# Moving a filter check into a hand-ordered instruction table, and giving the first tables a tile of their own

## The chip, the cores and the metric

The kernel runs on one core of one Trainium2 chip, as a single launch. The metric is the device time of the launch in microseconds (us). Engines are named as in the profile: PE (matmul), PEld (its weight loads), DVE (vector), ACT (scalar), POOL (gpsimd) and SP, whose queue issues most of the DMAs.

## The reference, cut to what matters

Two layers work on `x` of 4 x 32 images of 128 x 128, in float32. Four images are the batch, 32 the tokens.

```python
x = x + L0_conv(_ln_c(x))     # attention over 32 tokens, 16 heads, in a truncated Fourier basis,
                              # then two spectral mixers with instance norms
t = tokens(x)
t = t + L0_ffn(_ln_t(t))      # sigmoid recurrence over 128*128 rows, with batch statistics
x = from_tokens(t)
x = x + L1_conv(_ln_c(x))     # below
t = tokens(x)
t = t + L1_ffn(_ln_t(t))

def _ln_c(v):
    return (v - mean(v, -1)) / sqrt(var(v, -1) + 1e-6)

def _L1_conv_ref(x, bias, up_filter, dn_filter):
    x = x + bias
    x = repeat(repeat(x, 2, axis=2), 2, axis=3)
    x = conv_same(x, up_filter)               # 12 x 12 taps
    x = leaky_relu(x, 0.2) * sqrt(2)
    x = conv_same(x, dn_filter)               # 12 x 12 taps
    return x[:, :, ::2, ::2]
```

The two filters come in as 12 x 12 arrays. The kernel's convolution stage uses them as products of a column and a row. `filters()` checks on the chip that each filter is such a product (the result goes to `ok`, which is read at the end and would start a general path, not used here) and writes the one-dimensional taps to a small DRAM tensor `hankel`, from which the convolution stage builds its band matrices.

## The kernel before

**Stages.** The image array `XA` stays in SBUF (8 MB). In order of time:

- 0 to 137 us: loading, the row statistics and normalisation of `_ln_c`, the transform of every image to 32 x 17 coefficients, the scores of the attention and their softmax. There are eight steps `k`, each half a batch image set (16 tokens of one batch entry): `stats(k, n)` (DVE `bn_stats` L823, then `row_stats` L382 to L390, `rsqrt_of` L372 to L380, `p_n` at L829), `normalise` (ACT L845, DVE L847), `transform(k)` (PE L862 with the table of columns, L870 and L874/L876 with the tables of rows), then `scores` (ps_fr L895, FK L902, the products KM L909, psc L936) and `attend` (L1001 to L1020). Normalised images are stored to DRAM (`normed`, L881) and loaded again at L1071.
- 137 to 200 us: sums over tokens (`pm` L1092, `df` L1286), then norms.
- 200 to 449 us: the mixers, in eight chunks of four tokens.
- 449 to 505 us: the first recurrence; then the convolution stage, and the second recurrence with the output.

**Tables of constants.** `cst` is one tile of 128 partitions. SP loads it with two DMAs: the first 354 columns (`C_E`, `C_DW`, `C_CR`, which the transform uses) at L590 after two loads of `x`, the other 713 columns at L604 after two more. After them come the other loads of `x`, then `md` (a small bounce through DRAM that replicates the query-key weights, L653 and L655), and further weights.

**The one-column instruction.** `ndcm` (L717) is 1 - `dcm`, one column of the second part of `cst`. It is written in `weights()` after a piece of its own, and the scheduler put it between L379 and L380 of the first statistics.

**Orders.** Inside `with in_order():` every engine runs its instructions in the order in which the program makes them; outside (steps k = 2 to 7) a scheduler chooses. `SUMS`, `NORMS`, `MIXERS` are tables of names `piece.chunk`, run inside `in_order()`. The pieces of the mixers that matter here:

- `Z` (L1418, DVE: reads the first mixer's inverse from PSUM), `g` (L1423, ACT: gelu), `ST` (L1429, PE), `A` (L1434, ACT), `PF` (L478, PE, 32 matmuls), `ZS` (L1453, DVE statistics of Z), `ZD` (L1457 to L1459, DVE)
- `M1`, `PS`, `M2`, ..., `M4c` (L1565, L1566, DVE: the coefficients `G`), `FHG` (L491, PE: 64 small matmuls on `G`), `GB`/`gBc` (L1553, L1556), `IRI`/`IRS` (L506, PE), `TA` (L1579, PE), `R` (L1586 and L1587, DVE: the residual sums into `XA`)
- `FS` (L1597, DVE statistics for the first recurrence), `AF` (eight small operations from L1609, on POOL for most chunks; for the last chunk two `row_stats` of eight columns on DVE), `PW` (L1622, POOL power), `AO` (L1626), `XN`, `XT`, `XC`, `WX`, `BN` (the recurrence's inputs)

A name with two numbers, as `R1b.2`, is a part of a piece and its chunk. Bank "t" of the PSUM pool `psf` has one buffer, which `PS`, `GB` and `XT` take in turn.

**The filters before.** `filters()` (L739 to L808) is a generator of nine pieces, two times four and a DMA. Each half is: five DVE operations on 7 partitions (`fsq` to `frows`, L759 to L765); two matmuls `ps_f` on PE (L769, L770) and the copy `sums` on DVE (L772); eight DVE operations (`total` to `ok`, L775 to L785); six or seven (`fv` to `taps`, L789 to L805). The ninth is the POOL DMA `hankel<-taps` (L807). It was run as `extra` among the pieces of the last batch's scores:

```python
for work in (scoring, extra, extra, extra, scoring, scoring, scoring, products, products, scoring, scoring,
             scoring, scoring, scoring, extra, extra, scoring):
    step(work)
through(scoring, extra, attend(NB - 1))
```

`big("ps_f")` takes one of three PSUM buffers that the scores share.

Of the kernel before, what the change touches and what calls it, by code (L numbers as in the profile page):

```python
# [32 lines left out]
P = 128  # L33
# [5 lines left out]
PAD = 3  # L39
# [115 lines left out]
    IRI0.2 M4b.1 de.1 M4c.1 FHG.1 gBc.1 g3.2 Z0.2 FS2.0 Z1.2 g2.2 QG0.1 FS1.0 FS0.0 g1.2 g0.2 ST2.2 A2.2 sq2.2 FS3.0  # L155
    IRS0.1 TA1.1 ZS2.2 AF.0 sq3.2 ST0.2 QG1.1 PW.0 ZS3.2 ZD.2 A0.2 TA0.1 PF.2 sq0.2 R1a.1 sq1.2 LD2.1 FZ.2 SQ.2
    R0b.1 R0a.1 FHIa.3 R1b.1 AO.0 IRS2.1 M1.2 TA2.1 LD0.2 FHIb.3 R2b.1 XN1a.0 XN0b.0 PS.2 M2.2 TA3.1 QI0.3 XN0a.0
    PG1.2 XN1b.0 QI1.3 R2a.1 PG2.2 XT0.0 M2b.2 IRI2.3 R3a.1 R3b.1 XC0.0 XT1.0 P2.2 IRI0.3 Z2.3 M3.2 Z3.3 WX0.0 XC1.0
    P3.2 XN2a.0 al.2 Z0.3 M4a.2 g2.3 M4b.2 g3.3 Z1.3 g0.3 de.2 GB.2 M4c.2 BN0.0 g1.3 FS2.1 FS1.1 ZS2.3 ST2.3 sq1.3
    sq2.3 FHG.2 ST0.3 QG0.2 XN3b.0 IRS0.2 A2.3 A0.3 TA1.2 gBc.2 TA0.2 XN2b.0 FS3.1 PF.3 sq0.3 FS0.1 WC0.0 XT2.0  # L160
    ZS3.3 QG1.2 sq3.3 WX1.0 FZ.3 ZD.3 R1b.2 AF.1 R0b.2 IRS2.2 SQ.3 TA3.2 XC2.0 PW.1 R0a.2 PG1.3 R1a.2 M1.3 BN1.0
    LD2.2 PS.3 TA2.2 R3a.2 XN3a.0 WC1.0 M2.3 AO.1 WX2.0 R2a.2 FHIa.4 BN2.0 R3b.2 PG2.3 XN0b.1 FHIb.4 M2b.3 XT3.0
    P2.3 XN0a.1 M3.3 WC2.0 al.3 QI0.4 R2b.2 QI1.4 P3.3 XC3.0 IRI0.4 XN1a.1 XT0.1 Z1.4 M4a.3 IRI2.4 WX3.0 XN1b.1 Z0.4
    XC0.1 g1.4 M4b.3 de.3 g0.4 M4c.3 Z3.4 Z2.4 GB.3 FHG.3 BN3.0 FS3.2 g3.4 FS1.2 FS2.2 LD0.3 QG0.3 ST0.4 g2.4 FS0.2
    gBc.3 A0.4 QG1.3 ZS3.4 ZS2.4 IRS0.3 sq1.4 TA1.3 sq2.4 ST2.4 LD2.3 R1a.3 TA0.3 A2.4 WC3.0 PF.4 R1b.3 XN2b.1 FZ.4
    AF.2 ZD.4 XT1.1 sq3.4 R0b.3 WX0.1 IRS2.3 PW.2 R0a.3 SQ.4 sq0.4 PG1.4 TA2.3 XC1.1 M1.4 PS.4 BN0.1 TA3.3 AO.2 M2.4
    M2b.4 R2b.3 XN3a.1 XN2a.1 WC0.1 XT2.1 FHIa.5 R3b.3 LD0.4 R3a.3 XC2.1 P2.4 XN3b.1 XN0b.2 M3.4 PG2.4 XN0a.2 P3.4
    FHIb.5 QI0.5 QI1.5 XT3.1 WX1.1 IRI0.5 al.4 R2a.3 XN1a.2 XC3.1 BN1.1 M4a.4 Z1.5 IRI2.5 de.4 WC1.1 M4b.4 M4c.4
    XN1b.2 FS0.3 GB.4 gBc.4 WX2.1 XT0.2 BN2.1 g1.5 XN2b.2 Z3.5 WC2.1 FHG.4 FS3.3 XC0.2 QG0.4 WX3.1 FS1.3 FS2.3 QG1.4
    LD2.4 XT1.2 XN2a.2 XN3a.2 IRS0.4 XC1.2 TA1.4 BN3.1 Z2.5 TA0.4 AF.3 g2.5 Z0.5 R1b.4 XT2.2 IRS2.4 g0.5 WC3.1  # L170
    FHIa.6 sq0.5 R1a.4 R0a.4 R0b.4 WX0.2 ZS2.5 PW.3 g3.5 ZS3.5 BN0.2 TA2.4 AO.3 FHIb.6 ZD.5 ST2.5 sq2.5 FS0.4 R2b.4
    XN3b.2 ST0.5 XC2.2 sq1.5 R2a.4 sq3.5 WC0.2 A0.5 TA3.4 WX1.2 R3b.4 BN1.2 A2.5 PF.5 QI0.6 IRI0.6 XN0a.3 R3a.4
    XN0b.3 XT3.2 Z0.6 WC1.2 FZ.5 SQ.5 M1.5 QI1.6 PG1.5 XC3.2 g0.6 Z1.6 IRI2.6 PS.5 Z2.6 M2.5 g1.6 WX2.2 Z3.6 g2.6
    g3.6 P2.5 BN2.2 M2b.5 M3.5 XN1a.3 XT0.3 FS2.4 PG2.5 P3.5 FS3.4 XC0.3 ST0.6 al.5 M4a.5 WC2.2 A0.6 ST2.6 de.5
    M4b.5 M4c.5 WX0.3 A2.6 BN0.3 XN1b.3 PF.6 ZS2.6 sq0.6 ZS3.6 sq3.6 FS1.4 GB.5 FZ.6 FHG.5 WC0.3 SQ.6 QG0.5 WX3.2
    sq2.6 AF.4 IRS0.5 TA0.5 PW.4 PG1.6 sq1.6 gBc.5 XT1.3 QG1.5 M1.6 XC1.3 LD0.5 ZD.6 BN3.2 TA1.5 R0a.5 XN2a.3 R0b.5
    PS.6 LD2.5 AO.4 IRS2.5 M2.6 XN3b.3 XN2b.3 TA3.5 WC3.2 XT2.3 P2.6 M2b.6 XN3a.3 WX1.3 XC2.3 R1a.5 PG2.6 XT3.3
    TA2.5 R1b.5 FHIa.7 FHIb.7 XN0a.4 R3a.5 BN1.3 M3.6 R2a.5 XN0b.4 XC3.3 WC1.3 WX2.3 XN1b.4 QI0.7 R2b.5 XT0.4 P3.6
# [12 lines left out]
    XC22.7 WX20.7 BN20.7 WC00.7 WC02.7 WX22.7 BN22.7 WC20.7 WC22.7
# [15 lines left out]
C_E = 0  # L207

C_DW = C_E + 130
C_CR = C_DW + 96  # L210
C_SW = C_CR + 128
C_EH2 = C_SW + 256
# [19 lines left out]
def _constants():  # L232
    c = np.zeros((P, C_N), np.float64)
# [16 lines left out]
    c[:, C_E + 64 : C_E + 128] = rows.real.T @ basis  # L250
    c[:, C_E + 128 : C_E + 130] = (rows.imag.T @ basis)[:, :2]
# [3 lines left out]
    c[:, C_CR : C_CR + 64] = cols.real  # L255
    c[:, C_CR + 64 : C_CR + 128] = -cols.imag
# [30 lines left out]
def _network(  # L287
# [94 lines left out]
    def row_stats(st, n, mean, var):  # L382

        d = sm([P, NG], "rw_d")[:, :n]
        tt(mean, st[:, :, 1], st[:, :, 4], ALU.add)
        ts(mean, mean, 0.5, None, ALU.mult)
        tt(d, st[:, :, 1], st[:, :, 4], ALU.subtract)
        stt(d, d, 0.25, d, ALU.mult, ALU.mult)
        tt(var, st[:, :, 2], st[:, :, 5], ALU.add)
        stt(var, var, 1.0 / P, d, ALU.mult, ALU.add)  # L390
# [169 lines left out]
    s4 = aw.tile([P, NB], F32, name="s4")  # L560
    ndcm = aw.tile([P, 1], F32, name="ndcm")
# [28 lines left out]
    nc.sync.dma_start(cst[:, :C_SW], consts[:, :C_SW])  # L590
# [6 lines left out]
    if redo is not None:  # L597
        for k in range(2):
            F = wp.tile([2 * PAD + 1, 2, 12], F32, name=f"F{k}")
            taps_in.append(F)  # L600
            for j in range(2):
                f = up[j, 0] if k == 0 else dn[j]
                nc.gpsimd.dma_start(F[:, j, :], f[P // 2 - PAD : P // 2 + PAD + 1, :, P // 2])
    nc.sync.dma_start(cst[:, C_SW:], consts[:, C_SW:])  # L604
# [10 lines left out]
    def weights():  # L615
# [101 lines left out]
        ts(ndcm, dcm, -1.0, 1.0, ALU.mult, ALU.add)  # L717
# [21 lines left out]
    def filters():  # L739

        n = 2 * PAD + 1
# [4 lines left out]
        taps = wp.tile([1, 8, n], F32, name="taps")  # L750
        for k in range(2):
            F = taps_in[k]

            def small_(shape, name):
                return wp.tile(shape, F32, tag=name, name=name)


            fsq = small_([n, 3, 12], "fsq")
            tt(fsq[:, 0, :], F[:, 0, :], F[:, 1, :], ALU.add)  # L759
            tt(fsq[:, 1:3, :], F, F, ALU.mult)  # L760
            tt(fsq[:, 1, :], fsq[:, 1, :], fsq[:, 2, :], ALU.add)
            rsum = small_([n, 2], "rsum")
            nc.vector.tensor_reduce(rsum, F, AX.X, ALU.add)
            rows = small_([n, n, 2], "frows")
            tt(rows, ident[0:n, 0:n].unsqueeze(2).broadcast_to([n, n, 2]),  # L765
               rsum.unsqueeze(1).broadcast_to([n, n, 2]), ALU.mult)
            yield True
            p = big("ps_f")
            mm(p[:n, 0:24], ones_sq[0:n, 0:n], fsq[:, 0:2, :].rearrange("p a b -> p (a b)"), start=True, stop=True)  # L769
            mm(p[:n, 24 : 24 + 2 * n], ones_sq[0:n, 0:n], rows.rearrange("p a b -> p (a b)"), start=True, stop=True)  # L770
            sums = small_([n, 24 + 2 * n], "sums")
            nc.vector.tensor_copy(sums, p[:n, : 24 + 2 * n])  # L772
            yield True
            total = small_([n, 2], "total")
            nc.vector.tensor_reduce(total, sums[:, :24].rearrange("p (a b) -> p a b", a=2), AX.X, ALU.add)  # L775
            bound = small_([n, 1], "bound")
            tt(bound, total[:, 0:1], total[:, 0:1], ALU.mult)
            stt(bound, bound, FILTER_TOL * FILTER_TOL, total[:, 1:2], ALU.mult, ALU.mult)
# [1638 lines left out]
```

## Time and profile before

| what | us |
|---|---|
| median of 3 runs (lowest, highest) | 869.35 (868.36, 869.44) |
| profiled execution, its own time | 870.38 |
| its span | 868.6 |
| PE, DVE, ACT, POOL busy | 750.8, 710.9, 649.4, 361.2 |
| mean granted TensorE clock | 0.939 |

| stretch, us | length | PE | DVE | ACT | POOL | DMA share |
|---|---|---|---|---|---|---|
| 0 to 137 | 137 | 94.09 | 95.73 | 81.23 | 8.41 | 0.81 |
| 137 to 200 | 63 | 51.01 | 55.54 | 41.18 | 4.26 | 0.38 |
| 200 to 449 | 249 | 214.59 | 211.66 | 192.27 | 106.80 | 0.25 |
| 449 to 505 | 56 | 51.69 | 52.67 | 52.74 | 0.65 | 0.01 |

The tables are read so: the profile is of one execution, whose own time is 1.78 us more than its span; the second table has the busy time of each engine in a stretch, in us. A timeline line gives start, length, engine, line of the program, operation, output and inputs, shapes and count; in brackets at its end is the idle time of that engine just before it, and what ended that. A chain of waits follows the last instruction back to what released it at each step.

### The profile page before, as it was taken

Reading aid. Unit: us, or ns where it says so; the run is one execution under the profiler, and the core shown is the slowest. Engines: PE = TensorE matmul, PEld = TensorE weight load, DVE = VectorE, ACT = ScalarE, POOL = GpSimd, SP = SyncE. Lnnn points to the kernel's source line nnn. Section 1 sums busy time; section 2 is a strip of 40 time slices with the busy share of each in tenths; the row PEclk is TensorE's granted clock in tenths of the full one; section 3 lists DMA queues with packets and bytes.
Section 4 is the critical chain, followed back from the end, with each engine's and each line's share of the span. In section 5 each row is a group of like instructions: output and inputs, shape, how many; then the busy total and the mean of one; then the engine's idle time right before and its main releaser. Section 6 shows DMA issues by size and latency. Waiting matters only on the chain.

```text
span 868.6 us, 31057 instructions
## 1 busy us (share of the span) xinstructions
PE 750.8 (86%) x12550; PEld 560.5 (65%) x12550; DVE 710.9 (82%) x2330; ACT 649.4 (75%) x1669; POOL 361.2 (42%) x604
## 2 busy tenths in 40 slices
PE   1799967977878999899779979999999999998994
PEld 1566633336645555645349968888788877875994
DVE  3789668976598899899889978977878877677996
ACT  2588934585738689989779977887777887776994
POOL 2000000011435444365310016788788786961263
PEclk9799967996789899999999969999999999999998
DMA  9954992349611011120000000111111111118454
GB/s 224 260 153 94 250 366 103 137 204 276 162 51 49 26 49 35 42 73 25 25 1 1 1 3 17 40 41 40 28 41 28 41 28 40 40 40 291 172 186 148
DMA packets 105130, 83.22 MB, mean 96 GB/s; under 512 B 5457, under 2 KB 98129, under 8 KB 102865
## 3 DMA queue, kind: packets, MB, share of 16 engines
q1 hardware_dynamic: 104641, 80.86, 31.2%
q8 instruction: 101, 1.65, 0.8%
q0 software_dynamic: 288, 0.01, 0.2%
q14 instruction: 52, 0.43, 0.2%
q10 hardware_dynamic: 48, 0.26, 0.1%
HBM read 47.46 MB, written 33.66 MB: 93 GB/s over the span
## 4 chain that ended last, share of the span: by engine, by line
PE 44%; DVE 25%; ACT 14%; POOL 9%; issue 5%; DMA 1%; SPq 1%; DVEq 0%; ACTq 0%; POOLq 0%
PE ps_k L2068 5%; PE ps_scan L1915 4%; DVE XA L1587 4%; PE ps_d L2198 4%; ACT WXY L1917 4%; DVE XA L1586 4%; PE ps_st L862 3%; ACT yw L1917 3%; POOL XN L2047 3%; PE pm L1092 3%; PE ps_st L1429 3%; PE ps_r L2068 2%; PE ps_e L2205 2%; PE ps_y L1299 2%; POOL xn L2047 2%
## 5 line engine op out<-in xcount | busy, mean ns | idle before, releaser
L2188 DVE SCALAR_TENSOR_TENSOR U<-raw 128x512 f32<-128x512 f32 x128 | 89.8, 731 | 27.8 <-ACT raw L2180 27.6
L1916 DVE SCALAR_TENSOR_TENSOR ps_scan<-WXY,bs,ps_scan 128x128 f32<-128x128 f32 x376 | 105.5, 352 | 1.8 <-PE ps_scan L1915 0.8
L2068 PE MATMUL ps_k<-WXY,q 64*64 64x134 f32 x2048 | 86.0, 282 | 0.9 <-ACT WXY L2152 0.3
L2180 ACT COPY raw<-ps_k 128x512 f32<-128x512 f32 x128 | 71.0, 597 | 17.0 <-PE ps_k L2068 14.6
L2198 PEld LDWEIGHTS ps_d<-WXY,U 128*64 128x64 f32 x2048 | 66.7, 137 | 19.5 <-issue 12.1
L2047 POOL TENSOR_SCALAR XN<-XA,c_r,c_o 128x128 f32<-128x128 f32 x120 | 74.7, 631 | 5.0 <-issue 2.2
L2047 POOL TENSOR_SCALAR xn<-XA,f_r,f_o 128x128 f32<-128x128 f32 x120 | 67.2, 569 | 18.1 <-PE ps_x L2068 12.1
L2198 PE MATMUL ps_d<-WXY,U 128*64 128x67 f32 x2048 | 73.4, 224 | 1.2 <-ACT q L2211 0.9
L2068 PEld LDWEIGHTS ps_k<-WXY,q 64*64 64x64 f32 x2048 | 60.7, 135 | 6.4 <-DVE U L2188 0.8
L862 PE MATMUL ps_st<-cst,XA 128*128 128x130 f32 x256 | 42.8, 313 | 24.9 <-ACT XA L845 22.1
L2068 PE MATMUL ps_r<-WXY,XN 64*64 64x134 f32 x1024 | 59.0, 290 | 2.8 <-DVE XN L2047 1.3
L862 PEld LDWEIGHTS ps_st<-cst,XA 128*128 128x128 f32 x256 | 35.9, 212 | 29.1 <-ACT XA L845 23.1
L1644 ACT ACTIVATE xn<-XA,f_o,f_r 128x128 f32<-128x128 f32 x120 | 51.0, 489 | 4.6 <-DVE f_o L1626 3.4
L1423 ACT ACTIVATE Z<-Z,k,aB 128x128 f32<-128x128 f32 x128 | 51.0, 480 | 4.2 <-DVE Z L1418 4.0
L1586 DVE SCALAR_TENSOR_TENSOR XA<-ps_inv,r1B,xin 128x128 f32<-128x128 f32 x128 | 44.1, 345 | 8.1 <-PE ps_inv L1579 8.1
L1587 DVE SCALAR_TENSOR_TENSOR XA<-Z,gB,XA 128x128 f32<-128x128 f32 x128 | 46.3, 362 | 5.0
L2166 ACT COPY q<-ps_r 128x512 f32<-128x512 f32 x64 | 38.2, 597 | 13.2 <-PE ps_r L2068 12.8
L2027 POOL TENSOR_TENSOR c_r<-c_e,neg_half 128x16 f32<-128x16 f32 (+2 forms) x10 | 25.6, 2563 | 53.3 <-DVE c_e L2020 53.1
L506 PE MATMUL ps_inv<-invq,cst 64*128 64x512 f32 x128 | 41.4, 674 | 3.9 <-ACT invq L497 3.2
L456 PE MATMUL ps_wx<-xt,wvt 128*128 128x512 f32 x64 | 35.9, 643 | 6.7 <-ACT WXY L463 5.5
L845 ACT ACTIVATE XA<-XA,p_n,p_r 128x128 f32<-128x128 f32 x80 | 35.4, 491 | 7.6 <-DVE p_n L829 7.6
L2205 PE MATMUL ps_e<-WXY,q 128*64 128x67 f32 x1024 | 40.8, 222 | 0.0
(441 smaller groups left out, 2100.8 us busy)
## 6 DMA issues: line engine op xcount, KB each, us to landing
XA<-in_x_dram SPq DMA_DIRECT2D x16, 512.0 KB, 7.2
normed<-XA SPq DMA_DIRECT2D x8, 1024.0 KB, 6.1
XA<-normed SPq DMA_DIRECT2D x8, 1024.0 KB, 10.4
mixed<-XA SPq DMA_DIRECT2D x8, 1024.0 KB, 3.8
XA<-mixed SPq DMA_DIRECT2D x32, 256.0 KB, 5.3
xin<-in_x_dram SPq DMA_DIRECT2D x32, 256.0 KB, 3.3
turned<-XA SPq DMA_DIRECT2D x32, 256.0 KB, 2.5
out_dram<-res SPq DMA_DIRECT2D x52, 128.0 KB, 2.1
```

Source lines behind the costliest of these rows:

```text
L862: mm(p[:, i, :], XA[:, b, t0 + j + i, :], cst[:, C_E : C_E + 130], start=True, stop=True)
L1423: nc.scalar.activation(z, z, AF.Gelu, bias=k1, scale=aB[:, j : j + 1])
L1586: stt(a, p2[c, b][:, i], r1B[:, j : j + 1], xin[c, b - b % 2][:, b % 2, i], ALU.mult, ALU.add)
L1587: stt(a, Z[c][:, b, i], gB[c][:, n : n + 1], a, ALU.mult, ALU.add)
L1916: stt(p4, WX[:, :, h, :], s[:, 0:1], p4, ALU.mult, ALU.add)
L1917: nc.scalar.activation(dst, p4, AF.Sigmoid, bias=s[:, 1:2])
L2047: e.tensor_scalar(dst, src_, r, o, ALU.mult, ALU.add)
L2068: m = mm(dst, data, taps, start=(n == 0 and (i, j) not in last), stop=(n == 1), skip_group_check=True)
L2180: nc.scalar.copy(raw[u, k], banks["k", u][:, k])
L2188: stt(U[u][:, k].rearrange("p k s m -> p (k s m)"), v, SLOPE, v, ALU.mult, ALU.max)
L2198: mm(p[HALVES[s], m, b, REACH[k]], U[v][:, b, k, s, HALVES[m]], DR[:, k, REACH[k]], start=(m == 0 and b == 0 and k == 0), stop=(k == 1), s ...
L2205: mm(p[HALVES[j], b * P : b * P + P][:, REACH[m]], q3[v - 1][:, m, b, HALVES[j]], DC[:, m, REACH[m]], start=(b == 0 and m == 0), stop=(m = ...
```

## The change

Four things change.

1. The transform's tables get a tile of their own, `tables` (354 columns), loaded where `cst`'s first part was loaded. `cst` no longer has them, but keeps copies of 64 and 96 of the columns that the mixers use too; it is 873 columns in one DMA at the place of the second (436.5 KB for 356.5 KB).
2. `ndcm` is made inside the ordered block, behind the rest of the statistics of step 1. On DVE it stands after L832 of that step.
3. `row_stats` makes its sum, its difference and its sum of variances first, and then the three operations that use them. Steps 0 and 1 and the two groups of the last chunk have this new order on DVE; the others had it by the scheduler, or run on POOL.
4. `filters()` goes from the scoring to the mixers: its nine pieces are the entries `FL.0` of the table, run by the same order. Its PSUM buffer is bank "t"; two small tiles are put in memory of another. The zeros of `hankel`, with the clearing of `ok`, are outside the generator, ahead of it: on SP's queue the DMA `hankel<-fzero` goes from behind `m1d` to ahead of `md`, and one store of `normed` goes from ahead of `dd` to behind `m1d`.

Apart from these, each engine's order is the one before.

```diff
+C_F = 0
+C_FW = C_F + 130
+C_CR = C_FW + 96
+C_EARLY = C_CR + 128
+C_SW = 0
+C_E = C_SW + 256
+C_DW = C_E + 64
...
 def row_stats(st, n, mean, var):
         tt(mean, st[:, :, 1], st[:, :, 4], ALU.add)
+        tt(d, st[:, :, 1], st[:, :, 4], ALU.subtract)
+        tt(var, st[:, :, 2], st[:, :, 5], ALU.add)
         ts(mean, mean, 0.5, None, ALU.mult)
-        tt(d, st[:, :, 1], st[:, :, 4], ALU.subtract)
         stt(d, d, 0.25, d, ALU.mult, ALU.mult)
-        tt(var, st[:, :, 2], st[:, :, 5], ALU.add)
         stt(var, var, 1.0 / P, d, ALU.mult, ALU.add)
...
+    tables = aw.tile([P, C_EARLY], F32, name="tables")
...
-    nc.sync.dma_start(cst[:, :C_SW], consts[:, :C_SW])
+    nc.sync.dma_start(tables, consts[:, C_N:])
...
-    nc.sync.dma_start(cst[:, C_SW:], consts[:, C_SW:])
+    nc.sync.dma_start(cst, consts[:, :C_N])
...
-        ts(ndcm, dcm, -1.0, 1.0, ALU.mult, ALU.add)
         hermitian(...)
...
-    def filters():
-        n = 2 * PAD + 1
+    if redo is not None:
         zeros = wp.tile([P, 16], F32, name="fzero")
         nc.gpsimd.memset(zeros, 0.0)
         nc.sync.dma_start(hankel.rearrange("a (b c) -> (a b) c", c=16), zeros)
         nc.gpsimd.memset(ok, 0.0)
...
-                    mm(p[:, i, :], XA[:, b, t0 + j + i, :], cst[:, C_E : C_E + 130], start=True, stop=True)
+                    mm(p[:, i, :], XA[:, b, t0 + j + i, :], tables[:, C_F : C_F + 130], start=True, stop=True)
...
             through(ahead)
+            ts(ndcm, dcm, -1.0, 1.0, ALU.mult, ALU.add)
             ahead = stats(2, 2)
...
-            for work in (scoring, extra, extra, extra, scoring, scoring, scoring, products, products, scoring, scoring,
-                         scoring, scoring, scoring, extra, extra, scoring):
+            for work in (scoring, scoring, scoring, scoring, products, products, scoring, scoring, scoring, scoring):
                 step(work)
-            through(scoring, extra, attend(NB - 1))
+            through(scoring, attend(NB - 1))
...
+        filtering = filters(m1, lambda name: psf.tile([P, 512], F32, tag="t", name=name))
+        def FL(c, k):
+            next(filtering)
```

In the table (only the surroundings of the nine entries; they are numbered here, all are `FL.0` in the program):

```diff
+ ... M4b.1 de.1 M4c.1 FL(1) FHG.1 gBc.1 FL(2) g3.2 Z0.2 FS2.0 Z1.2 g2.2 ...
+ ... A0.2 TA0.1 PF.2 FL(3) sq0.2 R1a.1 ...
+ ... M2b.2 IRI2.3 R3a.1 FL(4) R3b.1 ...
+ ... GB.2 M4c.2 FL(5) BN0.0 g1.3 FS2.1 FS1.1 ZS2.3 ...
+ ... FS3.1 PF.3 FL(6) sq0.3 FS0.1 WC0.0 XT2.0 ZS3.3 QG1.2 sq3.3 WX1.0 FZ.3 ZD.3 R1b.2 ...
+ ... M2.3 AO.1 WX2.0 R2a.2 FL(7) FHIa.4 ...
+ ... g0.4 M4c.3 FL(8) Z3.4 ...
+ ... WC3.0 PF.4 FL(9) R1b.3 ...
```

## Prediction

> **What bounds the kernel now.** I read the page first (span, chain by engine), then the timelines of the places that the diff touches, the chain of waits and the busy time by stretch. The profiled execution took 870.38 us, 1.78 us around its span of 868.6; the median of the runs is 869.35. The working is made against 870.38, and the difference is then added to the median. About 0.2% (1.74 us) is what a measurement of this kernel can tell from no change.
>
> ```profile
> span 868.6 us, 31057 instructions
> PE 44%; DVE 25%; ACT 14%; POOL 9%; issue 5%; DMA 1%; SPq 1%; DVEq 0%; ACTq 0%; POOLq 0%
> 290.00:345.00 55.00, 50.11 (x517) 28.41 (x518) 51.19 (x176) 45.88 (x125) 27.97 (x64) 1.00 0.14 40
> ```
>
> No engine carries the span alone, so an edit is worth what its own stage makes of it. The third line is the busy time of PE, PEld, DVE, ACT and POOL in the middle of the mixers: DVE 51.19 of 55. Its timeline lists no idle time of DVE between 291.07 and 362.44, so what is put into DVE's queue there lengthens the stage.
>
> **Part A, the start.** Timeline, first 18 us:
>
> ```profile
> 12.07 0.17 DVE L379 TENSOR_TENSOR rq_d<-rq_d,rq_e 128x16 f32<-128x16 f32 x1
> 17.07 0.15 DVE L717 TENSOR_SCALAR ndcm<-cst 128x1 f32<-128x1 f32 x1 [4.82 <-DMA cst<-in_consts_dram]
> 17.14 0.28 DVE L380 SCALAR_TENSOR_TENSOR p_r<-rq_d,p_r 128x16 f32<-128x16 f32 x1
> 17.46 0.17 DVE L829 SCALAR_TENSOR_TENSOR p_n<-p_m,p_r 128x16 f32<-128x16 f32 x1
> 17.67 1.65 ACT L845 ACTIVATE XA<-XA,p_n,p_r 128x128 f32<-128x128 f32 x4 [6.12 <-DVE p_n L829]
> ```
>
> The one-column ndcm stands between two steps of the first statistics and waits 4.82 us for the second table transfer, which the statistics don't need. ACT's normalise and the first matmul (18.22) wait behind it. In the changed kernel ndcm comes after the statistics of k=1. The later copy of the same steps shows dependent distances of 0.21 (34.19, 34.40, 34.61 for p_n, 34.82 for ACT): from 12.07, p_n falls at 12.49 and ACT at 12.70, 4.97 earlier. The new order of the statistics puts the three independent operations side by side, which are 0.08 to 0.11 apart where dependent ones are 0.2 apart: 10.09 to 11.12 becomes about 0.77, 0.26 less. **Gain 5.2.**
>
> What is late next: the early tables are 177 KB at the same place in SP's queue, issued at 1.84 to 3.34 before the second pair of x loads, which land by 8.41: in time for 13. The second table transfer grows by 80 KB, 0.3 us at the 263 GB/s of 12 to 46 us. The zeros of `hankel` go ahead of `md` in SP's queue; SP ends the eight x loads at 25.63, so `md` can't start earlier and may start 0.6 to 1.9 later (SP's issue of a small transfer such as `dd` took 0.62, of an x load 14.91/8 = 1.9). Its copies, issued to 32.98 and landing 5.6 later at 38.6, come by 40.5 and are needed at 49.67 - 5.2 = 44.5 (L909): hidden by 4. The last load of batch 1 I estimate to land at 24.0 to 24.5, needed at about 23.8; those statistics are ready at 30.42 but ACT takes them at 33.45, so that is hidden by 3. One `normed` store moves behind `m1d`, where the zeros' issue took 11.76; no one reads it before 136.8, after loads issued at 111.64. Bounds for A: 3 to 5.3; I take 5.2, since all next-late transfers have cover.
>
> **Part B, the end of scoring.** Timeline:
>
> ```profile
> 127.81 1.51 PE L936 MATMUL psc<-KT,FQ 96*32 96x128 f32 x24
> 129.57 0.18 DVE L772 COPY sums<-ps_f 7x38 f32<-7x38 f32 x1 [2.26 <-PE ps_f L770]
> 131.94 0.24 DVE L805 COPY taps<-fv 1x14 f32<-1x14 f32 x2
> 132.10 0.27 DVE L1001 TENSOR_TENSOR Pm<-wqk,pg 128x128 f32<-128x128 f32 x1
> 132.40 0.29 DVE L1002 TENSOR_TENSOR Pm<-Pm,psc 128x128 f32<-128x128 f32 x1
> ```
>
> The scores end at 129.32, but the filter's second half keeps DVE until 132.10, and then the softmax, L1020 and M's first matmul (136.83) follow one by one. Without it L1001 runs early and L1002 starts at 129.4 to 129.5: 2.9 to 3.0. In the first half (113.9 to 120.5) its operations lie between the softmax's, and its matmuls ahead of ps_fr and in one of three shared banks; DVE's FK copy at 121.12, on which the rest hangs, comes about 1.1 earlier by ps_fr's second pair (118.80) starting behind the first instead of waiting for the bank. **Gain 4.0** (2.9 to 4.2).
>
> **Part C, last statistics.** The new order also serves the last chunk's two groups of six (430.16 to 431.13 and 440.98 to 441.95); 0.22 each, the second ahead of POOL's f_r at 442.26. **Gain 0.4.** The row: 441.18 to 441.26 for two independent operations, 441.26 to 441.46 for dependent ones. [...]
>
> **Part D, nine pieces in the mixers.** On DVE each half is 5, then 1 copy, 8 and 6 or 7 operations; rows of before give 0.72 (126.59 to 127.31), 0.18, 1.51 (129.79 to 131.30) and 1.01 (125.58 to 126.59) for the first half, 0.80 (131.30 to 132.10) for the second. The copy of `sums` also waits for two matmuls of ps_f on PE, which executes in order.
>
> ```profile
> 253.75 0.22 DVE L1566 TENSOR_SCALAR G<-G 128x128 f32<-128x128 f32 x1
> 254.48 3.15 PE L491 MATMUL ps_inv<-cst,G 32*64 32x128 f32 x64
> 254.58 0.75 DVE L1418 SCALAR_TENSOR_TENSOR Z<-XA,sc,ps_inv 128x512 f32<-128x512 f32 x1 [0.60 <-PE ps_inv L506]
> 258.17 3.19 ACT L1423 ACTIVATE Z<-Z,k,aB 128x128 f32<-128x128 f32 x8
> 264.36 0.35 DVE L1586 SCALAR_TENSOR_TENSOR XA<-ps_inv,r1B,xin 128x128 f32<-128x128 f32 x1 [1.26 <-PE ps_inv L1579]
> ```
>
> Pieces 1 to 3. ps_f stands on PE behind those 64 matmuls (free at 257.56), the copy 0.32 later (129.25 to 129.57) at 257.9, and behind it in DVE's queue is Z0.2, which so moves from 254.58 to 258.0, and with it Z1.2, statistics and the rest. ACT's gelu on Z1.2 (258.17) comes at 260.25, TA0.1 ends on PE 1.4 later. Piece 3 then adds 1.51, part of it in the gaps 0.35 and 1.26 that the trace shows before L1586. The second pair of L1586 comes at 267.5 where it came at 264.36: **+3.15**. Piece 4, in an unbroken stretch of L1586/L1587: **+1.0**. Piece 5 (0.72) falls into the gap of 3.40 that the next lines show: 0; with that cover gone it would cost 0.7.
>
> ```profile
> 287.48 0.20 DVE L1459 TENSOR_TENSOR SQ<-zd,zst 128x16 f32<-128x16 f32 x1
> 291.07 0.35 DVE L1586 SCALAR_TENSOR_TENSOR XA<-ps_inv,r1B,xin 128x128 f32<-128x128 f32 x1 [3.40 <-PE ps_inv L1579]
> 291.82 1.08 PE L478 MATMUL ps_pf<-A,cst 128*32 128x128 f32 x32
> ```
>
> Piece 6: its ps_f stands behind the 32 matmuls of PF.3, so the second copy can't run before 293.2. Behind it on DVE are now FS0.1 (0.82), ZS3.3 (0.9) and ZD.3 (0.6), which had run before 287.7, ahead of the gap, and then L1586. R1b.2 starts at about 295.6 for 291.07: **+4.5**. Piece 7 **+1.55**, piece 8 **+0.8** in the full stretch; piece 9 is a DMA issue on POOL (0.56 before) in its idle time. Sum **+11.0**; from 9.5 (if the gaps of 1.15 and 0.45 after 362 take some) to 11.5.
>
> A price against it that the rows show: of 39 L1587 (two SBUF inputs) between 285 and 345, three took 0.57 to 0.63 for 0.35, all beside short POOL operations. The pieces have 19 such operations: 19 x 3/39 x 0.25 = 0.4, which I leave to the upper end. [...]
>
> **Sum:** -5.2 - 4.0 - 0.4 + 11.0 = +1.4: 871.7 for a profiled execution, **870.7** for the median. What is won at the start and in scoring is given back by two waits put ahead of work that was early.
>
> **Rivals.**
> 1. *The waits of pieces 2 and 6 are absorbed* (faster). For it: between 251.96 and 263.40 the chain runs on PE, not DVE, and DVE sat idle 3.40 before 291.07. Then the pieces cost their busy time, 0.72 + 0.18 + 1.51 + 1.01 + 0.18 + 1.55 + 0.80 = 5.95: net -3.7, **865.7**. Against: the work behind the copy is 2.3 us that used to fill that time, and what follows has no idle time. It decides if R1b.2 comes less than 2 later than piece 5's stretch.
> 2. *The start's gain is lost to a transfer* (slower). DMA's busy share is 1.13 between 12 and 46; a first half 5.2 earlier asks for the same loads from a queue that issues no sooner. If the last load of batch 1 or batch 2's loads arrive 3 later than they are now needed, A is 2: net +4.6, **873.9**. It decides once DVE's wait on an x load passes the 3 us of cover. Against: only the first loads show such a wait now (5.6 in two).
> 3. *The change doesn't do what it says at the start*: the first matmul still waits for a table transfer. A is 0, net +6.6, **876**. Against: DVE reaches ndcm's new place near 29.7 and the tables' queue place is early.
>
> **How the numbers follow.** Forecast 0.57 (own range 868.0 to 873.2), rival 1 0.20, rival 2 0.18, rival 3 0.05. Faster by over 0.2% (under 867.6): nearly all of rival 1 and little of the forecast, 0.22. Slower (over 871.1): 0.38 of the forecast, nearly all of 2 and 3: 0.44. Same: 0.34. Range 865.2 to 874.6 takes in rivals 1 and 2, with the port's price above.
>
> **What would show it.** Right: the first L845 of ACT at 12.4 to 12.7; M's first matmul at 127 to 128; Z0.2 idle before `sums` about 3 on PE ps_f; a second such idle of over 4 before the other `sums`; the last mixer piece about 1.4 later than before. Wrong: an idle DVE `st` on an x load over 3; ps_f's wait under 1; or L1586 gaps that shrink as the copies come.

## The result, and the profile after

The changed kernel takes 876.36 us (median of 8 runs, 873.70 to 881.76) where the kernel before takes 870.09 (8 runs, 868.36 to 873.16): a ratio of 1.0059, with an interval of 1.003 to 1.0088. It is slower, and the time lies above the range of the prediction.

The profiled execution that the following lines come from took 876.6 us. The same program was profiled twice more (873.2 and 872.97), and the kernel before once more (870.38 again). The page of the changed kernel, span and chain of waits by engine:

```profile
span 874.8 us, 31055 instructions
PE 38%; DVE 25%; ACT 12%; POOL 7%; issue 4%; SPq 0%; DVEq 0%; ACTq 0%; POOLq 0%
```

The chain's shares can't be held against before's (44, 14 and 9% for PE, ACT and POOL): those add up to 99% of the span, these to 86%, since this chain can be followed back only to 116.7 us. Nothing in these two lines says why the span grew by 6.2. The places that the diff touches do. First the timeline of the start:

```profile
12.09 0.17 DVE L385 SCALAR_TENSOR_TENSOR p_r<-rq_d,p_r 128x16 f32<-128x16 f32 x1
12.30 0.18 DVE L769 SCALAR_TENSOR_TENSOR p_n<-p_m,p_r 128x16 f32<-128x16 f32 x1
12.51 1.65 ACT L785 ACTIVATE XA<-XA,p_n,p_r 128x128 f32<-128x128 f32 x4 [1.16 <-DVE p_n L769]
13.06 2.97 PE L802 MATMUL ps_st<-tables,XA 128*128 128x130 f32 x12 [13.06 <-ACT XA L785]
```

The wait of 4.82 for the table is gone. ACT's first normalise starts at 12.51 (forecast: 12.4 to 12.7) and the first matmul at 13.06 for 18.22. The end of scoring, timeline of DVE:

```profile
121.27 0.29 DVE L941 TENSOR_TENSOR Pm<-wqk,pg 128x128 f32<-128x128 f32 x1
124.99 0.29 DVE L942 TENSOR_TENSOR Pm<-Pm,psc 128x128 f32<-128x128 f32 x1 [3.43 <-PE psc L876]
```

L942 (L1002 before) now waits for the scores alone, and comes 7.41 earlier than before's 132.40. The first copy of `sums` in the mixers, timeline of DVE:

```profile
246.34 0.22 DVE L1566 TENSOR_SCALAR G<-G 128x128 f32<-128x128 f32 x1
250.43 0.19 DVE L1292 COPY sums<-ps_f 7x38 f32<-7x38 f32 x1 [3.24 <-PE ps_f L1290]
250.55 0.72 DVE L1418 SCALAR_TENSOR_TENSOR Z<-XA,sc,ps_inv 128x512 f32<-128x512 f32 x1
```

Z0.2 (the third line) came 0.83 after G's operation before, and now comes 4.21 after it, behind a wait of 3.24 for the two matmuls of ps_f. The second copy, timeline of DVE:

```profile
281.85 0.84 DVE L1597 BATCH_NORM_STATS2 f_st<-XA 128x6 f32<-128x128 f32 x4
290.05 0.18 DVE L1292 COPY sums<-ps_f 7x38 f32<-7x38 f32 x1 [7.36 <-PE ps_f L1290]
290.17 0.85 DVE L1597 BATCH_NORM_STATS2 f_st<-XA 128x6 f32<-128x128 f32 x4
292.42 0.34 DVE L1586 SCALAR_TENSOR_TENSOR XA<-ps_inv,r1B,xin 128x128 f32<-128x128 f32 x1
```

DVE stands still for 7.36, with FS0.1, ZS3.3, ZD.3 and R1b.2's L1586 queued behind the copy. L1586 starts at 292.42 for 291.07. Since everything was 7.42 early at before's 247, this stretch lost 8.8.

To see where the time goes I laid the traces side by side: for each DVE instruction that two traces share, its start in the one less its start in before's first profile. The columns are times in that profile (us); below zero is earlier than before. The experiments of the next section are in the same table.

```
profile                        18      42      67     136     247     290     316     447     457     856
after                        -5.16   -5.60   -2.53   -7.41   -7.42   +1.33   +4.65   +4.92   +6.21   +6.21
after_again                  -5.39   -5.76   -6.67  -10.22  -11.05   -1.85   +1.49   +1.46   +2.74   +2.84
after_third                  -5.27   -5.75   -4.91   -9.34   -9.31   -1.85   +1.47   +1.19   +2.48   +2.68
before_again                 +0.20   +0.02   -0.83   -0.86   -0.85   -0.87   -0.86   -0.85   -0.87   -0.27
e1_start_only                -5.04   -5.16   -6.09   -5.98   -6.11   -6.14   -6.14   -6.66   -5.53   -5.14
e3_filters_only              -0.11   +0.15   +0.15   -3.97   -6.64   +2.10   +5.43   +5.89   +7.16   +7.49
e2_no_copy_waits             -5.05   -5.52   -4.69   -9.11   -9.03   -7.25   -4.84   -5.21   -3.94   -3.60
e4_first_wait_only           -5.28   -5.10   -5.15   -9.29   -9.82   -2.30   +0.31   +1.41   +3.77   +4.55
c1_filters_in_transform      -5.05   -4.43   -4.16   -7.13   -7.46   -8.42   -8.42   -9.09   -9.10   -8.64
c2_filters_in_gaps           -4.81   -5.28   -4.45   -8.88   -8.33   -9.42   -9.38  -10.21  -10.22  -10.73
c2w_warm_start (c2 again)    -5.35   -4.69   -4.74   -8.85   -8.71  -10.08  -10.03  -10.13   -8.90   -8.70
w_filler_matmuls             -5.36   -4.26   +1.58   -2.84   -2.29   -3.39   -3.34   -4.07   -4.07   -3.86
```

Three things stand out in the first three rows, which are one program. The mixers' nine pieces cost 11 to 13 in all of them (from column 247 to 316: 12.1, 12.5, 10.8). Another 1.3 is lost between 447 and 457. And the three differ most between 42 and 67, though they are one program: the first profile loses 3.07 of its lead there and the second gains 0.91.

### The profile page after: what moved, and what is told of

Its sections match the earlier page's. It is cut to its first block, busy times and chain, and to the rows that moved or that the text cites. A ratio compares the mean times of both kernels' runs of the same rounds, so it can differ in the third digit from the quotient of the medians.

```text
span 874.8 us, 31055 instructions
## 1 busy us (share of the span) xinstructions
PE 761.5 (87%) x12550; PEld 568.2 (65%) x12550; DVE 711.1 (81%) x2330; ACT 650.1 (74%) x1669; POOL 361.1 (41%) x604
## 4 chain that ended last, share of the span: by engine, by line
PE 38%; DVE 25%; ACT 12%; POOL 7%; issue 4%; SPq 0%; DVEq 0%; ACTq 0%; POOLq 0%
PE ps_scan L1920 6%; DVE XA L1587 5%; PE ps_k L2073 5%; PE ps_d L2203 4%; DVE XA L1586 4%; ACT WXY L1922 4%; POOL XN L2052 3%; PE pm L1031 3%; PE ps_r L2073 2%; DVE f_st L1597 2%; PE ps_e L2210 2%; PE ps_y L1238 2%; PE ps_st L1429 2%; ACT Z L1423 2%; POOL xn L2052 2%
## 5 line engine op out<-in xcount | busy, mean ns | idle before, releaser
L2052 POOL TENSOR_SCALAR xn<-XA,f_r,f_o 128x128 f32<-128x128 f32 x120 | 67.2, 569 | 18.2 <-PE ps_x L2073 12.1
L802 PE MATMUL ps_st<-tables,XA 128*128 128x130 f32 x256 | 46.4, 336 | 18.8 <-ACT XA L785 16.6
L802 PEld LDWEIGHTS ps_st<-tables,XA 128*128 128x128 f32 x256 | 39.7, 234 | 22.7 <-ACT XA L785 19.6
L1586 DVE SCALAR_TENSOR_TENSOR XA<-ps_inv,r1B,xin 128x128 f32<-128x128 f32 x128 | 44.0, 344 | 4.9 <-PE ps_inv L1579 4.8
L461 PE MATMUL ps_wx<-xt,wvt 128*128 128x512 f32 x64 | 39.5, 702 | 6.3 <-ACT WXY L468 5.1
L1920 PE MATMUL ps_scan<-y,wvt 128*128 128x128 f32 x246 | 40.4, 281 | 0.0
```

Of the source, the lines that this page charges most:

```text
L802: mm(p[:, i, :], XA[:, b, t0 + j + i, :], tables[:, C_F : C_F + 130], start=True, stop=True)
L1586: stt(a, p2[c, b][:, i], r1B[:, j : j + 1], xin[c, b - b % 2][:, b % 2, i], ALU.mult, ALU.add)
L1920: mm(p4, self.t[:, 1, :], prev, start=True, stop=True)
L2052: e.tensor_scalar(dst, src_, r, o, ALU.mult, ALU.add)
```

## Experiments

The theory after the result: the waits of the two copies cost what was forecast, and the rest is TensorE's granted clock: 0.57 between 41 and 53 in the changed kernel's first profile for 1.00 in before's, and 0.84 between 285 and 306 for 0.94. That it changes with when and how often PE is idle is a guess of mine, not something the traces show. The rivals: the start's gain is lost to a transfer, or the pieces cost their place in DVE's queue with or without waits.

**The start alone.** `filters()` goes back ahead of attention, with the pools and the schedule of before; the early tables, the placed ndcm and the order of the statistics stay.

```diff
-            for work in (scoring, scoring, scoring, scoring, products, products, ...
+            for work in (scoring, extra, extra, extra, scoring, scoring, scoring, products, ...
-    ... M4c.1 FL.0 FHG.1 gBc.1 FL.0 g3.2 Z0.2 ...   (and the other seven entries)
+    ... M4c.1 FHG.1 gBc.1 g3.2 Z0.2 ...
```

> The changed kernel with the nine filter pieces back in the scoring, where the kernel before had them; the start (own tile for the early tables, ndcm late, order of the statistics, zeros of hankel early) stays. Theory 1: the start is worth 5.2 us at the first matmul (13.06 for 18.22), and what of it is left at the first matmul of the sums is set by how long TensorE's granted clock is at half between 13 and 60 us: 134.3 for 136.83 with the half-clock stretch of 41.4 to 51.6 that the changed kernel's trace has, 131.6 without one; 1.5 to 5.7 faster than the kernel before with the 0.4 of the last statistics, and no change of distance inside scoring or mixers. Rival: the early start is worth nothing or less in total (transfers or the clock take all of it): within 1 of the kernel before or slower.

Measured: 865.21 (863.72 to 867.70), ratio 0.9924 (0.9896 to 0.9951). The row of the table holds at -6 from 67 to 345; the last statistics add 0.5 (-6.14 to -6.66); 1.13 is lost between 447 and 457. So no transfer takes the gain of the start: the same loads and table transfers as in the changed kernel leave it at 5 to 6 here. By the ratio this kernel is 6.6 us faster than before, where 1.5 to 5.7 was expected.

**The filter's pieces without the start.** The changed kernel with ndcm at its old place:

```diff
+        ts(ndcm, dcm, -1.0, 1.0, ALU.mult, ALU.add)
         hermitian(...)
...
             through(ahead)
-            ts(ndcm, dcm, -1.0, 1.0, ALU.mult, ALU.add)
             ahead = stats(2, 2)
```

> The changed kernel with ndcm made where the kernel before made it, so that the first statistics wait for the table transfer again or the normalise on DVE does; the filter pieces stay in the mixers. Theory 1 (the loss is the pieces in the mixers, 12.3 in the changed kernel's trace against 4.9 won in scoring): 5 to 8 us slower than the kernel before, with both waits of the sums copy (3.2 and 7.4 before) there again. Rival (the loss comes from the early start shifting TensorE's half-clock stretches over the rest): at most 3 slower.

Measured: 880.96 (877.86 to 882.32), ratio 1.0097 (1.0064 to 1.013). The timeline of DVE, start of this kernel, shows the removed wait back in full, and the normalise behind it:

```profile
17.46 0.15 DVE L723 TENSOR_SCALAR ndcm<-cst 128x1 f32<-128x1 f32 x1 [5.18 <-DMA cst<-in_consts_dram]
17.79 0.33 DVE L788 TENSOR_SCALAR XA<-XA,p_r,p_n 128x128 f32<-128x128 f32 x1
```

From 67 to 136 it gains 4.12 (forecast for the end of scoring: 4.0), and from 247 to 316 it loses 12.1. By the ratio it is 8.4 us slower than before (expected 5 to 8). The two halves of the change nearly add: by the ratios -0.76% and +0.97% make +0.21%, against +0.59% for the whole, and the intervals overlap.

**No wait at either copy.** The two matmuls of ps_f and the copy of `sums` become two entries of the table, so that other work stands between them on DVE:

```diff
             mm(p[:n, 24 : 24 + 2 * n], ...)
+            yield True
             sums = small_([n, 24 + 2 * n], "sums")
...
-    ... A0.2 TA0.1 PF.2 FL.0 sq0.2 ...
+    ... A0.2 TA0.1 PF.2 FL.0 FL.0 sq0.2 ...
-    ... PF.3 FL.0 sq0.3 ... XC2.0 PW.1 R0a.2 PG1.3 R1a.2 M1.3 ...
+    ... PF.3 sq0.3 ... XC2.0 FL.0 PW.1 R0a.2 PG1.3 R1a.2 FL.0 M1.3 ...
```

The first copy now stands after PF.2, no longer ahead of Z0.2, and the second after R1a.2, behind the L1586 that it held up.

> The changed kernel with the sums copies split from their matmuls in the table: the first copy stands ahead of piece 3, behind PF.2; the second half's matmuls stand behind XC2.0 and its copy behind R1a.2. All else is the changed kernel. Theory 1: each copy waits under 0.5 us, Z0.2 and FS0.1, ZS3.3, ZD.3 run early as before, and the mixers cost 4 to 5 us instead of 12.3: 867.5 to 870.5. Rival (the pieces' busy time and the clock are what costs, and the waits only use time that DVE would wait anyway later): 873 or more.

Measured: 866.54 (865.61 to 870.52), ratio 0.9947 (0.9922 to 0.9971). The timeline of DVE in this kernel, around both copies:

```profile
252.20 0.18 DVE L1293 COPY sums<-ps_f 7x38 f32<-7x38 f32 x1
...
283.83 0.35 DVE L1587 SCALAR_TENSOR_TENSOR XA<-ps_inv,r1B,xin 128x128 f32<-128x128 f32 x1 [2.76 <-PE ps_inv L1580]
...
289.61 0.18 DVE L1293 COPY sums<-ps_f 7x38 f32<-7x38 f32 x1
```

Neither copy has idle time before it, the old gap before R1b.2 is back (2.76), and from 247 to 316 the pieces cost 4.2 where the changed kernel pays 10.8 to 12.5. The instructions are the same; only the place of two matmuls and two copies differs. The difference, 6.6 to 8.3, is the price of the two waits and of what follows from them.

**One wait alone.** As above, but with the first half's matmuls and copy ahead of Z0.2 again:

```diff
-    ... gBc.1 FL.0 g3.2 Z0.2 ... PF.2 FL.0 FL.0 sq0.2 ...
+    ... gBc.1 FL.0 FL.0 g3.2 Z0.2 ... PF.2 FL.0 sq0.2 ...
```

> The changed kernel with only the second wait taken out: the second half's matmuls stand behind XC2.0, its copy behind R1a.2; pieces 2 and 3 are where the change put them. Theory 1: the first copy waits 3.2 us and costs about 2.5 to 3.3 by the third piece (0.7 to 0.8 in the kernel without the waits), the second wait is gone, and the mixers cost 6 to 6.8 in place of 12.3 to 12.5: 868 to 871 and halfway between the changed kernel and the one without both waits. Clock part: with the second wait gone, the stretch of half clock that the changed kernel has near 294 to 305 isn't there, and pieces 7 and 8 cost 2.3 and not 3.1 to 3.3. Rival (the waits use the same idle time, and one of them alone costs as much as both): 873 or more.

Measured: 869.54 (866.20 to 875.01), ratio 0.9994 (0.997 to 1.0017). By the ratios, the first wait costs 0.47% (4.1 us) over no wait, the second another 0.65% (5.7); the intervals leave each some 3 to either side. The chain of waits of DVE by releaser (kernel with one wait; us, times, longest):

```profile
DVE sums L1293 <- PE ps_f L1290: 4.2, 2, 3.8
```

The profile of this kernel is a warning. It is of the second slowest of the ten runs (874.8), and from 247 to 316 it loses 10.1, where 6 to 6.8 was expected. With the second wait gone it still lost 2.2 (-4.52 to -2.30) between 286 and 291. The busy time by stretch (us, then busy time of PE, PEld, DVE, ACT and POOL with counts, PE's granted clock, DMA share, GB/s), first of this kernel and then of the one without waits:

```profile
276.00:290.00 14.00, 14.00 (x99) 9.86 (x103) 8.04 (x40) 9.90 (x32) 4.85 (x10) 0.52 0.01 1
```

```profile
276.00:290.00 14.00, 13.40 (x136) 8.43 (x128) 10.78 (x44) 9.77 (x31) 7.69 (x15) 0.85 0.01 1
```

PE was busy without a break at a granted clock of 0.52 and got through 99 matmuls where the other got through 136. A stretch at half clock, at a place where PE sets the pace, cost as much here as the second wait did in the third profile of the changed kernel (2.2 over the same instructions).

**The pieces elsewhere.** First in the filter's old pool and banks, stepped through in the later `transform(k)` loops:

```diff
             ts(ndcm, dcm, -1.0, 1.0, ALU.mult, ALU.add)
+            step(extra)
...
-                step(ahead, prepare if k > 2 else None, scoring, softmax if k > 5 else None)
+                step(ahead, ..., softmax if k > 5 else None, extra if k > 5 else None)
...
-        through(softmax, prepare)
+        through(softmax, prepare, extra)
```

> The changed kernel with the filter pieces taken out of the mixers and put beside the transform of the last batch (steps 6 and 7, where DVE was busy 12.36 of 22 us between 90 and 112), the first five operations behind ndcm. Theory 1: scoring keeps its 4 to 5 us, the start its 2.5 to 5, the mixers lose their 12.3, and the pieces lie in DVE's idle time: 861 to 864. Rival (between 90 and 112 DVE's operations are on the chain of the softmaxes of the earlier batches, so pieces there cost what they save in the scoring): 866 to 869.

Measured: 866.02 (861.46 to 869.47), ratio 0.9924 (0.990 to 0.9947). The profile is of the fastest of the twelve runs. In it the lead of 4.16 at 67 shrinks where the pieces stand and is gone for a moment at before's 101 us (+0.24); at 113 it is 2.83 again. By 136 it is 7.13, a gain of 2.97 since 67 where the changed kernel gains 3.6 to 4.9, so that most of what the pieces cost is made good, and the mixers lose nothing (-7.46 to -8.42). Between theory 1 and its rival the times don't decide: the median is the rival's, while the ratio, taken of before's 870.09, makes 863.5, which is theory 1's. Then with the split copy, at gaps that before's trace shows in the first mixer stages:

```diff
-    ... HR.0 IRI0.0 Z0.0 ... ST0.0 ZS2.0 ... ZD.0 Z1.1 ... SQ.0 M1.0 ... M2.0 Z2.1 ... PG2.0 M3.0 ... SQ.1 QG0.0 ...
+    ... HR.0 FL.0 IRI0.0 Z0.0 ... ST0.0 FL.0 FL.0 ZS2.0 ... ZD.0 FL.0 FL.0 Z1.1 ... SQ.0 FL.0 M1.0 ...
+    ... M2.0 FL.0 Z2.1 ... PG2.0 FL.0 M3.0 ... SQ.1 FL.0 QG0.0 ... TA1.0 FL.0 R1b.0 FL.0 sq0.1 ...
```

> The changed kernel with the pieces, copies split from matmuls, moved forward in the mixers' table to where the trace shows DVE idle between 204 and 240 us: behind HR.0, ST0.0, ZD.0 (two), SQ.0, M2.0, PG2.0, SQ.1, TA1.0 and R1b.0. Theory 1 (what costs is DVE's queue where it has no idle time, not the number of operations): the mixers cost 0 to 1 us, scoring keeps 4 to 5, the start 2.5 to 6: 860 to 863. Rival (the small operations and the shared bank cost wherever they are): 866 or more.

Measured: 862.64 (860.31 to 863.78), ratio 0.9917 (0.9897 to 0.9937). It beats both kernels. A timeline of DVE in this kernel shows why:

```profile
197.70 2.71 DVE L1419 SCALAR_TENSOR_TENSOR Z<-XA,sc,ps_inv 128x512 f32<-128x512 f32 x4
203.08 0.18 DVE L1293 COPY sums<-ps_f 7x38 f32<-7x38 f32 x1 [2.67 <-PE ps_f L1290]
203.68 2.22 DVE L1454 BATCH_NORM_STATS2 zst<-Z 128x6 f32<-128x128 f32 x8 [0.41 <-ACT Z L1424]
```

One copy still waits 2.67, but the next operation then waits 0.41 more for ACT. The timeline of DVE in the kernel before has the same operation, with this idle time ahead of it:

```profile
212.56 2.22 DVE L1453 BATCH_NORM_STATS2 zst<-Z 128x6 f32<-128x128 f32 x8 [3.26 <-ACT Z L1423]
```

2.67, 0.18 for the copy and 0.41 make these 3.26: the wait covers a stall that was there anyway, and the shift is -8.52 at 197, -8.33 at 247 and -9.42 at 290. A wait of about the same length cost the changed kernel 3 at 247.

That the pieces cost nothing here rests on the profiles. By the ratios this kernel is only 0.6 us ahead of the start alone (0.9917 for 0.9924), where the profiles put the end of scoring at some 4; the intervals leave about 3 to either side.

**The same program again.** To see what belongs to the program and what to the execution, the changed kernel and the kernel before were each profiled again, unaltered:

> The changed kernel unaltered, for another profile of the same program. Clock theory: the early gain of 5 to 6 us at 41 us is lost in part wherever TensorE is granted half its clock before 70 us, and those stretches fall differently from one execution to the next: the shift of the M stage against the kernel before's trace is between -7.4 (with 10.2 us at half clock there) and -10.5 (with none), and the time differs from 876.6 by as much as the half-clock stretches do; the two waits of the sums copies come back within 0.5 of 3.2 and 7.4. Rival (a transfer in the new start takes it): the shift at 67 us is -2.5 again whatever the clock.

> The kernel before unaltered, for another profile. Clock theory: its time between the same two events differs from its first trace only in stretches whose granted clock differs; up to 4 us in total. Rival (the trace of before is typical and its spread is elsewhere): all stages within 0.5 us of the first trace.

> The changed kernel unaltered, a third profile. Clock theory: mixers 12.3 to 12.5 again with waits of 3.2 and 7.4 at the two copies, half clock somewhere between 290 and 306; the shift at 67 us between -2.5 and -6.7, by 0.33 us for each us at half clock between 40 and 60.

The windows 41 to 53 and 285 to 306 of the first profile of before:

```profile
41.00:53.00 12.00, 10.19 (x131) 6.89 (x129) 10.55 (x48) 9.99 (x25) 0.68 (x3) 1.00 0.87 222
285.00:306.00 21.00, 19.02 (x189) 11.27 (x182) 16.59 (x61) 13.96 (x39) 12.10 (x27) 0.94 0.09 27
```

of the first profile of the changed kernel:

```profile
41.00:53.00 12.00, 11.52 (x115) 9.39 (x115) 12.00 (x45) 8.77 (x23) 0.65 (x3) 0.57 0.96 256
285.00:306.00 21.00, 14.80 (x138) 7.57 (x141) 14.30 (x53) 9.22 (x26) 10.34 (x23) 0.84 0.09 25
```

and of its second:

```profile
41.00:53.00 12.00, 11.29 (x89) 8.29 (x89) 12.00 (x44) 11.15 (x29) 1.90 (x3) 1.00 0.90 227
285.00:306.00 21.00, 14.42 (x141) 7.36 (x140) 17.21 (x66) 9.11 (x24) 11.38 (x26) 0.84 0.09 26
```

The last three columns are the granted clock, DMA share and GB/s. Between 41 and 53 the one program ran once at 0.57 and once at 1.00, and the DMA columns differ little. What the clock does is seen on the same matmuls, in timelines of PE; first profile, then second:

```profile
46.69 4.43 PE L802 MATMUL ps_st<-tables,XA 128*128 128x130 f32 x18
```

```profile
44.01 2.39 PE L802 MATMUL ps_st<-tables,XA 128*128 128x130 f32 x16
```

That is 0.246 for one against 0.149. Between 285 and 306 it is the other way round: both executions of the changed kernel have 0.84, and PE is busy for 14.8 and 14.4 of 21 where before it was for 19.0. That loss belongs to the program. The waits of DVE by releaser (us, times, longest) come back too: second profile, then third.

```profile
DVE sums L1292 <- PE ps_f L1290: 11.0, 2, 7.5
```

```profile
DVE sums L1292 <- PE ps_f L1290: 9.3, 2, 5.5
```

The third profile misses what was expected of it: its second wait is 5.5 for 7.4, and its mixers cost 10.8 for 12.3 to 12.5.

**A warm start.** Could the half-clock stretch near 45 be prevented by keeping PE busy from the beginning? The best kernel (pieces in the early gaps), first a second profile of it without any edit (it stands under the label c2w_warm_start, but its program is that of c2):

> The same program as c2, for a second profile of it: the shift at 67 us against its first trace goes with the half-clock stretches before 70 us (0.33 us for each us at half clock, from 3.5 lost in 10.2), and nothing else differs by over 0.5 us before 200 us.

It took 861.25, and, unlike its first profile, loses 1.23 between 447 and 457. Then with matmuls on a table of ones ahead of the first statistics:

```diff
         with in_order():
+            if redo is not None:
+                warm = big("warm")
+                for _ in range(56):
+                    mm(warm[:, :P], ones_sq, ones_sq, start=True, stop=True)
             through(stats(0, 1))
```

> The kernel with the pieces in the gaps (c2), and 56 matmuls of 128x128 on TensorE ahead of the first real one, from about 2 to 12 us, into a buffer that nobody reads. Clock theory: TensorE is at full clock by the first real matmul instead of 11 us later, so the transform of the first steps is shorter on PE; at 42 us the shift grows by 0.3 to 1, since there ACT and DVE bound as well. Rival: the first matmuls wait for the fillers or for the clock all the same, and the shift at 42 us is unchanged or smaller; the time is that of c2 within 1 us.

Measured: 862.30 (858.49 to 866.80), ratio 0.9892 (0.9858 to 0.9926), not to be told from the same kernel without them. A timeline of PE in this kernel, and two stretches:

```profile
1.23 15.30 PE L989 MATMUL warm<-ones_sq 128*128 128x128 f32 x112 [1.23 <-DVE ones_sq L549]
16.36 1.50 PE L802 MATMUL ps_st<-tables,XA 128*128 128x130 f32 x12
```

```profile
24.00:37.00 13.00, 9.87 (x54) 7.64 (x53) 10.49 (x59) 7.13 (x18) 0.00 (x0) 0.63 1.10 273
44.00:58.00 14.00, 13.40 (x69) 9.87 (x65) 14.00 (x51) 9.14 (x24) 0.58 (x3) 0.51 0.93 251
```

The filler (its 56 matmuls are 112 records in the trace) took 15.30, so the first real matmul came 3.3 later than in the changed kernel; the first twelve ran at twice the pace (1.50 for 2.97). But in this execution half-clock stretches came later and longer (44 to 58 at 0.51). The lead at 42 is 4.26 where c2's two profiles have 5.28 and 4.69 (0.3 to 1 more was expected), and at 67 it was gone (+1.58). The profiled execution is the slowest of the four: 866.80 at a mean granted clock of 0.934, for 858.49 to 863.51 at 0.942 and 0.943 in the others. So it isn't shown that the fillers bring the long stretch, and the four times show neither a gain nor a loss.

## Why the prediction was wrong

Step by step, in its own letters. The mechanism it forecast is the one that the runs show; the sum was too low, and it had no term for the clock.

- **A, the start (-5.2): right at the start, and kept by the program.** -5.16 at the first matmul, and at 67 -6.1 and -6.7 in the two profiles that have no half-clock stretch from 26 us to there (start alone, and the changed kernel's second). In the changed kernel's first profile 3.07 of it goes between 42 and 67, with a clock of 0.57 between 41 and 53. Rival 2 forecast a loss of this size here by a transfer. The size occurs, its mechanism doesn't: DVE's waits on x loads stayed at 5.3 at the longest (5.2 before), `md` moved by 1.73 without a wait, and the same program in its second profile lost nothing.
- **B, the end of scoring (-4.0): right.** -3.6 to -4.9 between 67 and 136 in the three profiles of the changed kernel, -4.12 with the filter alone. M's first matmul starts at 129.41, and in the other two profiles at 126.61 and 127.48 (forecast 127 to 128).
- **C, the last statistics (-0.4): right.** -0.5 where the start stands alone. The order of the statistics at the start took 0.78 for 1.03 (forecast 0.77).
- **D, the pieces (+11.0): the waits were right, the end of the stretch was low.** From 247 to 290: 8.75, 9.20 and 7.46, where the steps for pieces 1 to 6 make 3.15 + 1.0 + 0 + 4.5 = 8.65. The first wait is 3.2 to 3.8 (forecast about 3.4), the second 5.5 to 7.5. Piece 5 cost 0.65 after all (forecast 0, and 0.7 without its cover), piece 6 4.1, 4.2 and 2.2 (forecast 4.5): in the first two profiles these two misses nearly cancel. From 290 to 316, for pieces 7 and 8: 3.3 in all profiles with the second wait, where 1.55 + 0.8 = 2.35 was forecast. Without that wait the same pieces took 2.4 and 2.6, so the missing 0.9 goes with the wait. 0.8 of it lies at piece 7 (2.3 for 1.5). The timelines of PE and DVE in the changed kernel show it in three lines; the fourth is PE's in the kernel before:

```profile
299.84 0.57 PE L1478 MATMUL ps_st<-parts,cst 128*128 128x12 f32 x2 [5.92 <-DVE parts L1474]
300.57 2.08 PE L1579 MATMUL ps_inv<-XA,gI 128*128 128x512 f32 x2
302.69 0.35 DVE L1586 SCALAR_TENSOR_TENSOR XA<-ps_inv,r1B,xin 128x128 f32<-128x128 f32 x1 [0.74 <-PE ps_inv L1579]
298.80 1.12 PE L1579 MATMUL ps_inv<-XA,gI 128*128 128x512 f32 x2
```

Behind the second wait PE has nothing to do for 5.92 (1.86 before). Its clock falls to half meanwhile (297.3 to 304.1), the same two matmuls take 2.08 for 1.12, and DVE waits 0.74 for them. All four profiles with the second wait have the same: PE idle for 5.92 to 5.94, 2.08 for the two matmuls, a wait of 0.73 or 0.74. No other profile has a half-clock stretch of over 3.4 there, or this wait.
- **Rival 1, the waits are absorbed: refuted at this place, true at another.** R1b.2 came 7.5 to 9.2 later; in the early gaps one wait of 2.67 cost nothing. **Rival 3**, a first matmul that still waits for a table, falls with the start's 12.51.
- **The price of operations beside POOL** left to the upper end (0.4): not needed. Piece 3's eight operations took 1.50 in the mixers, beside a POOL operation of 2.95 that starts among them at 257.56, for 1.51 in scoring without one. That a port is behind this price, as its name in the prediction's range has it, no run shows; what the runs show in its place is these 1.50 for 1.51.
- **The step that failed** is "The working is made against 870.38, and the difference is then added to the median". It took the granted clock of one execution of before (0.939) over unchanged, and so put the clock's share at nothing, without a price or a spread. What the runs showed in its place: +0.9 at 294 to 305 (belongs to the second wait), +1.3 at 447 to 457, and from 42 to 67 between -0.9 and +3.1, by the execution. 1.4 + 0.9 + 1.3 is 3.6, and with the last 2.7 to 6.7; the three profiles stand at 6.2, 2.8 and 2.6 above before's first (the third has the shorter second wait), and the interval of the ratio allows 2.6 to 7.7.
- **The runs go with the clock.** Of the eight of the changed kernel, those with a mean granted clock of 0.937 and above took 873.70 to 876.12, those below 876.60 to 881.76. With the two later profiles five of ten executions lie inside the range of the prediction. At 0.937 to 0.942 the median of the changed kernel is 873.8 (6 executions) and that of before 871.2 (30 runs): 2.6 apart, nearer to the forecast 1.4. Below 0.937 are 4 of 10 and 6 of 49. The 0.2% that the prediction gave a measurement is too fine: before's eight runs alone spread over 0.55%.

Two things stay open. The first is the 1.3 at 447 to 457. It comes with a half-clock stretch at 443 to 462: seven profiles with 3.4 us of it lose 1.1 to 1.3 there, the one with 6.8 us (one wait alone) loses 2.4, and those without lose nothing. All three profiles of the changed kernel have it and neither of before; but the start alone has it too, and of two profiles of the best kernel one has it and one hasn't, so it isn't the pieces in the mixers that bring it. The second is what sets the clock down near 45 in some executions. Of the ten profiles with the early start six have a half-clock stretch that begins between 40 and 46, and of the three without it none; that the early start brings it is a rival that no run tests.

## What to carry to other kernels

In an order written by hand, a step that has a part on one engine and a part on another is two entries, not one: put the second where the engine reaches it after the first has run, or where it would have waited anyway. By the profiles the same instructions cost 11 to 13 us in one place, 4 with the two copies moved a little, and nothing in early gaps. When a forecast of half a per cent is made from one profile, profile the same program twice first, and give the clock's spread a term of its own.

## What the runs showed of the hardware

- **The clock has two steps here, and falls for multiples of about 3.4 us.** In the first profiles of the kernel before and of the changed kernel every record of it is 1 or a half, and the half-clock stretches last 3.4, 6.8, 10.2 or 13.7, and 23.9 (before) and 17.1 (changed) near 117, apart from the last, which the end of the trace cuts off.
- **What half clock costs in a kernel of mixed engines.** Between 42 and 67 the shift changes by -0.9 in the three profiles without a half-clock stretch between 30.8 and 67, by -0.05 to 0 in three with one of 3.4 us from 30 on, by +0.8 in three with two of 3.4, by +3.1 with 3.4 and 10.2 (the changed kernel, first profile) and by +5.8 with 6.8 and 13.7 (filler matmuls); the profile with the pieces in the transform, which differs there, is left out. From one step to the next that is 0.25 to 0.4 us for each us at half clock, and 0.33 to 0.38 at 447 to 457.
- **Independent small operations of DVE overlap in these rows.** The timeline of DVE in the changed kernel, the first statistics:

```profile
10.15 0.19 DVE L390 TENSOR_TENSOR p_m<-st 128x16 f32<-128x16 f32 x1
10.25 0.18 DVE L391 TENSOR_TENSOR rw_d<-st 128x16 f32<-128x16 f32 x1
10.35 0.18 DVE L392 TENSOR_TENSOR p_v<-st 128x16 f32<-128x16 f32 x1
```

Each starts 0.10 after the one before, which takes 0.18 to 0.19. Further on in the same statistics, operations that read the result of the one before start 0.20 and 0.21 apart (10.52, 10.72 and 10.93).
